# Band scores on tiles of two widths: blocks 1 and 2 as whole 128-key products

## The chip, the cores and the metric

The kernel runs on one core of a Trainium2 chip. Times are device microseconds of that core, the median of several executions; one more execution was taken with the hardware profiler, and all views of the profile come from it. PE is TensorE's matrix array (matmuls), PEld its weight loads, DVE VectorE, ACT ScalarE, POOL GpSimd, SP the engine that issues most transfers.

## The reference

The input x has the shape (2, 256, 128, 128): two items, 256 times, 128 bands, 128 channels, float32. Three residual steps follow each other, each on a layer normalization of x over the channels:

```
x = x + mha(ln(x) by time,  4 heads, causal mask over the 256 times)
x = x + mha(ln(x) by band,  4 heads, only bands at most 16 apart)
x = x + w2(gelu(w1(ln(x))))           # 128 -> 512 -> 128 channels
```

The second step is what the change touches. For each of 512 (item, time) pairs it takes 128 bands as queries and as keys. With 32 channels per head, the score of a query and a key is a dot product over 32 numbers. Scores of bands more than 16 apart are masked out before the softmax.

## The kernel before

The work is cut into groups of four blocks of 128 positions. There are three kinds: OverTime (128 groups, first), and then OverBands and FeedForward (128 groups each), which come in runs: eight OverBands groups, then their eight FeedForward groups, 16 runs in all. A group carries 512 columns of the transposed, normalized input xnT. Its stages are methods, and the loop in `run` (from line 1046) issues, for step n, the scores of group n, then the weighting (`weigh`) of group n-1, the output product of group n-2, and, for later groups, loads, statistics, normalization, and the query, key and value products. Thus a group passes through several steps, and each step of the loop mixes the stages of several groups.

The order of work on each engine is written out by hand: the class InOrder (line 860) passes each instruction to the engine and pins it to program order (line 870, which is why nearly every row of the profile names that line). So a late instruction holds up everything that stands behind it on its engine. PSUM is used as eight banks of 512 float32 columns, handed out in turn (`turn_of_bank`, line 903); a product whose bank is still being read waits for the reader.

The products run on parts of TensorE's array. A profile row such as "32*64 32x80" is a product on a tile of 32 rows and 64 columns of the array with 80 moving columns. The rows are the contraction: a head's 32 channels, so four heads sit on four row tiles. The columns are the weights' free size, here the keys. Most products of the kernel use 128*32: `product` (line 646) cuts the 128 output channels into four strips of 32. A float32 product leaves two LDWEIGHTS and two MATMUL records in the profile.

`OverBands.scores` (line 752) writes, per head, one bank with the keys on the partitions and the 512 queries of the four blocks along the columns. It works by halves of 64 keys: the first half of a block's keys reaches the block's queries 0 to 79, the second half the queries 48 to 127. The two corners that no product writes hold what stood in the bank earlier, and are masked out later. Per block there are eight products (two halves, four heads), in 32x64 tiles; per group 32.

After the scores come `first_function` (line 767): for head 3 VectorE takes the minimum with 60 and adds the band mask in place, in PSUM (`bank<-bank,band` in the profile), and ScalarE takes the exponential of each head's bank (`pf<-bank`). `first_mask` (line 777) clears, for heads 0 to 2, what lies outside the band on GpSimd. In the next step `weigh` (line 791) forms the sums of the exponentials (`bank<-pf,ones`) and the weighted values (`bank<-pf,v`); `divide` (line 615) on VectorE then inverts the sums (u) and gives oT. The next step's `output` multiplies by the output weights (`bank<-wn,oT`).

In the step after the last OverBands group of a run ("turn", line 1071) the first FeedForward group's hidden products (`bank<-xnT,w1f`) stand in front of that group's `weigh`.

The OverTime stage, which the change leaves alone, forms its scores in 32x128 tiles with 256 or 128 moving columns (`time_scores`, line 729).

Of the kernel before, what the change touches and what calls it, by code (L numbers as in the profile page):

```python
# [19 lines left out]
P = 128  # L20
H = 4
D = 32
BAND = 16
EPS = 1e-5
NEG = -1e38
NT = 4
# [6 lines left out]
HALF = P // 2  # L33
# [608 lines left out]
def rows_of(h):  # L642
    return slice(h * D, (h + 1) * D)
# [102 lines left out]
class OverBands(Attention):  # L746
# [5 lines left out]
    def scores(self, heads):  # L752
        path = self.path
        self.sp = {h: path.bank([P, NT * P], "sp") for h in heads}
        for i in range(NT):
            for e in range(2):
                keys = slice(e * HALF, (e + 1) * HALF)
                a = i * P + e * (HALF - BAND)
                q = slice(a, a + HALF + BAND)
                for h in heads:  # L760
                    r = rows_of(h)
                    path.tensor.matmul(
                        self.sp[h][keys, q], self.kT[r, i * P + e * HALF : i * P + (e + 1) * HALF], self.qT[r, q],
                        start=True, stop=True,
                    )

    def first_function(self):
# [451 lines left out]
```

## Time and profile before

| | |
|---|---|
| runs shown | median 2706.66 us of 3 (2705.89 to 2706.93) |
| the profiled execution's own time | 2703.05 us |
| its span | 2701.3 us |
| TensorE clock granted | 0.999 of full speed |
| OverTime groups, until the first band scores | 970 us |
| one run of eight OverBands and eight FeedForward groups | 107 to 108 us (the first 111) |

The span is the time between the first and the last instruction. A matmul record begins when the array starts on it; its end is modelled, and records of neighbouring products overlap. So the distance between the starts of two records tells more than their length. The idle time in brackets at the end of a timeline row is what the engine waited before it, with what released it.

### The profile page before, as it was taken

How to read it: one execution, taken by the hardware profiler on the slowest of the kernel's cores; microseconds unless marked ns; L12 is line 12 of the kernel's file. 1: busy time of each engine (PE TensorE's matmuls, PEld its weight loads, DVE VectorE, ACT ScalarE, POOL GpSimd, SP SyncE). 2: the span in 40 equal slices, each digit the busy share in tenths (PEclk: the TensorE clock that was granted, in tenths of full speed). 3: DMA queues.
4: the chain of work that ended last, by engine and by line, in shares of the span. 5: the costliest groups of instructions: out<-in, count | busy, mean ns of one | idle time of the engine just before them, and what ended most of it. 6: DMA issues, size and time to landing. Idle time of an engine off the chain costs nothing.

```text
span 2701.3 us, 148062 instructions
## 1 busy us (share of the span) xinstructions
PE 2662.7 (99%) x64566; PEld 1824.9 (68%) x64566; DVE 2280.2 (84%) x6708; ACT 1848.3 (68%) x3620; POOL 1868.7 (69%) x2169
## 2 busy tenths in 40 slices
PE   7999999999999999999999999999999999999998
PEld 5667666767676666666666666666666766666665
DVE  7999999999999997868769779688697796886874
ACT  6888888888888874655746646557456465565573
POOL 3888788878888886667657666666676666665762
PEclk9999999999999999999999999999999999999999
DMA  5555555555555535445444444454444444544433
GB/s 151 142 151 143 145 151 144 149 146 142 151 144 148 150 101 129 111 121 132 109 127 124 115 125 116 121 128 116 120 124 117 121 119 121 135 108 121 129 100 82
DMA packets 471477, 346.55 MB, mean 128 GB/s; under 512 B 43296, under 2 KB 405152, under 8 KB 470816
## 3 DMA queue, kind: packets, MB, share of 16 engines
q1 hardware_dynamic: 469568, 335.92, 47.8%
q8 instruction: 508, 8.32, 1.3%
q14 instruction: 153, 1.25, 0.2%
q10 hardware_dynamic: 1248, 1.05, 0.2%
HBM read 169.03 MB, written 167.77 MB: 125 GB/s over the span
## 4 chain that ended last, share of the span: by engine, by line
PE 83%; DVE 13%; DMA 2%; issue 1%; ACT 0%; SPq 0%; DVEq 0%; ACTq 0%
PE bank L870 83%; DVE xh L870 3%; DVE bank L870 3%; DVE stats L870 2%; DVE z L870 2%; DVE u L870 2%; DMA xnT<-turned 1%; DVE x L870 1%; DVE mv L870 1%; DMA turned<-z 0%; SPq L870 0%; DMA x<-in_x 0%; DVE oT L870 0%; DMA rows_sb<-in_rows 0%; ACT p L870 0%
## 5 line engine op out<-in xcount | busy, mean ns | idle before, releaser
L870 ACT ACTIVATE hT<-bank,b 128x512 f32<-128x512 f32 x512 | 347.1, 688 | 536.0 <-PE bank L870 517.0
L870 POOL TENSOR_SCALAR_AFFINE_SELECT pf<-pf 128x512 f32<-128x512 f32 x768 | 478.5, 638 | 246.8 <-ACT pf L870 220.5
L870 DVE TENSOR_SCALAR xh<-x,mv,rstd 128x160 f32<-128x160 f32 x1536 | 597.1, 431 | 14.2
L870 PEld LDWEIGHTS bank<-w2T_sb,hT 128*32 128x32 f32 x16384 | 459.7, 110 | 63.1 <-issue 38.8
L870 PE MATMUL bank<-xnT,wf 128*32 128x512 f32 x4096 | 488.6, 592 | 2.0 <-ACT p L870 2.0
L870 PE MATMUL bank<-w2T_sb,hT 128*32 128x128 f32 x16384 | 477.5, 273 | 0.5 <-ACT hT L870 0.2
L870 PE MATMUL bank<-xnT,w1f 128*32 128x512 f32 x4096 | 474.2, 592 | 0.0
L870 ACT ACTIVATE p<-bank 128x512 f32<-128x512 f32 (+1 forms) x1024 | 417.3, 499 | 15.1 <-PE bank L870 3.8
L870 POOL TENSOR_SCALAR_AFFINE_SELECT p<-p 128x1024 f32<-128x1024 f32 x256 | 280.9, 1097 | 188.2 <-ACT p L870 188.2
L870 DVE TENSOR_TENSOR res<-bank,res 128x512 f32<-128x512 f32 x256 | 171.1, 668 | 229.1 <-PE bank L870 227.2
L870 PE MATMUL bank<-qT,kT 32*64 32x80 f32 (+2 forms) x12288 | 346.9, 275 | 4.2 <-DVE oT L870 2.2
L870 PEld LDWEIGHTS bank<-wf,xnT 128*32 128x32 f32 x8192 | 235.5, 110 | 154.4 <-issue 135.9
L870 PEld LDWEIGHTS bank<-qT,kT 32*64 32x64 f32 (+1 forms) x12288 | 298.0, 148 | 58.7 <-ACT kT L870 48.2
L870 POOL TENSOR_TENSOR p<-p,p 128x512 f32<-128x512 f32 x256 | 329.2, 1286 | 10.7
L870 DVE BATCH_NORM_STATS2 stats<-x 128x6 f32<-128x128 f32 x1536 | 326.9, 275 | 0.9 <-DMA x<-in_x 0.9
L870 ACT ACTIVATE pf<-bank 128x512 f32<-128x512 f32 x512 | 267.1, 602 | 50.9 <-PE bank L870 48.8
L870 DVE STREAM_TRANSPOSE z<-xh 128x512 f32<-128x512 f32 x384 | 273.3, 712 | 13.4
L870 PEld LDWEIGHTS bank<-xnT,w1f 128*32 128x32 f32 x4096 | 156.4, 110 | 189.4 <-issue 159.3
L870 POOL TENSOR_SCALAR rstd<-mv 128x4 f32<-128x4 f32 x248 | 56.7, 229 | 312.8 <-DVE mv L870 311.3
L870 PE MATMUL bank<-wf,xnT 128*32 128x128 f32 x8192 | 272.6, 273 | 0.0
L870 PE MATMUL bank<-wn,oT 128*32 128x128 f32 x8192 | 271.7, 273 | 0.0
L870 POOL TENSOR_TENSOR rstd<-rstd,mhalf 128x4 f32<-128x4 f32 x248 | 257.0, 1036 | 20.7
(93 smaller groups left out, 3770.3 us busy)
## 6 DMA issues: line engine op xcount, KB each, us to landing
turned<-z SPq DMA_DIRECT2D x1536, 64.0 KB, 2.2
xnT<-turned SPq DMA_DIRECT2D x384, 256.0 KB, 3.1
x<-in_x SPq DMA_DIRECT2D x128, 256.0 KB, 4.1
x<-res SPq DMA_DIRECT2D x256, 128.0 KB, 2.4
x<-x SPq DMA_DIRECT2D x128, 256.0 KB, 4.2
out<-res SPq DMA_DIRECT2D x256, 128.0 KB, 2.5
w1T_sb<-in_w1T ACTq DMA_DIRECT2D x1, 256.0 KB, 6.5
w2T_sb<-in_w2T ACTq DMA_DIRECT2D x1, 256.0 KB, 7.9
```

The lines of the kernel that those rows point to most:

```text
L870: return self.tc.keep_in_program_order(emit(*args, **kwargs))
```

## The change

In blocks 0 and 3 of a group the scores are formed as before. In blocks 1 and 2 one product per head takes all 128 keys and all 128 queries of the block. These use tiles of 32 rows and 128 columns. A group then has 8 + 4 + 4 + 8 = 24 products, the four heads next to each other as before. No other engine's instructions, their order or their waits are edited.

```diff
     def scores(self, heads):
         path = self.path
         self.sp = {h: path.bank([P, NT * P], "sp") for h in heads}
-        for i in range(NT):
-            for e in range(2):
-                keys = slice(e * HALF, (e + 1) * HALF)
-                a = i * P + e * (HALF - BAND)
-                q = slice(a, a + HALF + BAND)
+        for i, part in ((0, HALF), (1, P), (2, P), (3, HALF)):
+            reach = 0 if part == P else BAND
+            for e in range(0, P, part):
+                a = i * P + (e - reach if e else 0)
+                q, keys = slice(a, a + part + reach), slice(i * P + e, i * P + e + part)
                 for h in heads:
                     r = rows_of(h)
                     path.tensor.matmul(
-                        self.sp[h][keys, q], self.kT[r, i * P + e * HALF : i * P + (e + 1) * HALF], self.qT[r, q],
-                        start=True, stop=True,
+                        self.sp[h][e : e + part, q], self.kT[r, keys], self.qT[r, q], start=True, stop=True
                     )
```

## The prediction

> **What bounds the kernel now.** I read the page first, then one steady step of the stage that is changed on TensorE and on VectorE, then two stages that already use what the change brings in. The page:
>
> ```profile
> span 2701.3 us, 148062 instructions
> PE 2662.7 (99%) x64566; PEld 1824.9 (68%) x64566; DVE 2280.2 (84%) x6708; ACT 1848.3 (68%) x3620; POOL 1868.7 (69%) x2169
> ...
> PE 83%; DVE 13%; DMA 2%; issue 1%; ACT 0%; SPq 0%; DVEq 0%; ACTq 0%
> ...
> L870 PE MATMUL bank<-qT,kT 32*64 32x80 f32 (+2 forms) x12288 | 346.9, 275 | 4.2 <-DVE oT L870 2.2
> ```
>
> TensorE sets the pace, VectorE takes 13% of the chain. But 99% busy does not say that PE streams all that time: a record lasts longer than the stream it stands for. The band scores are the 8,192 records of 32x80 (two for each float32 product, 64 for each of 128 groups). So I work with starts. The timeline of TensorE over one steady band step (start, length, form, count):
>
> ```profile
> 1535.81 1.09 PE L870 MATMUL bank<-qT,kT 32*64 32x80 f32 x64
> 1536.83 1.06 PE L870 MATMUL bank<-pf,ones 128*32 128x512 f32 x8
> 1537.71 1.06 PE L870 MATMUL bank<-pf,v 128*32 128x128 f32 x32
> 1538.59 1.06 PE L870 MATMUL bank<-wn,oT 128*32 128x128 f32 x32
> 1539.46 1.90 PE L870 MATMUL bank<-xnT,wf 128*32 128x512 f32 x16
> 1541.17 1.06 PE L870 MATMUL bank<-wf,xnT 128*32 128x128 f32 x32
> 1542.16 1.06 PE L870 MATMUL bank<-qT,kT 32*64 32x80 f32 x64
> ```
>
> A step is 6.35 us here; the mean of the like steps in the last 15 of the 16 runs of eight band groups is 6.324. 32 records of 128 columns take 0.88 us, four side by side in 0.109 or 0.110. Between record starts, from the last value product before the scores to the first product after them, pass 1.190 us in the mean (groups 3 to 6 of those runs; groups 0 to 2: 1.174, 1.187, 1.173).
>
> VectorE over the same step, the next one's first line included:
>
> ```profile
> 1537.32 0.69 DVE L870 SCALAR_TENSOR_TENSOR bank<-bank,band 128x512 f32<-128x512 f32 x1
> 1537.92 1.60 DVE L870 TENSOR_SCALAR xh<-x,mv,rstd 128x160 f32<-128x160 f32 x4
> ...
> 1543.24 0.69 DVE L870 TENSOR_TENSOR oT<-bank,u 128x512 f32<-128x512 f32 x1
> 1543.85 0.69 DVE L870 SCALAR_TENSOR_TENSOR bank<-bank,band 128x512 f32<-128x512 f32 x1
> ```
>
> No instruction in it has idle time before it: VectorE needs 6.53 us for a step, PE 6.32. So from the fourth group of a run VectorE falls behind. The band mask starts this long after the end of the scores, median of the 16 runs, groups 0 to 7: 0.14, 0.19, 0.21, 0.19, 0.42, 0.61, 0.83, 0.93 us. Group 7's scores then wait for banks (its stretch is 1.290 us, not 1.190), and PE waits in the turn to the feed-forward groups:
>
> ```profile
> 1562.93 0.64 PE L870 MATMUL bank<-pf,ones 128*32 128x512 f32 x4 [0.77 <-DVE u L870]
> ```
>
> Against the 430 ns of the pass before, that start is 0.95 us late; in all 16 turns 15.6 us.
>
> [...] A float32 product is two loads and two matmuls here, [...] in the group at 1510.58 us the first 32 score records run regularly and those after them come one product per about 26 ns, in steps of 17 and 42. [...]
>
> **The change, part by part.** Blocks 0 and 3 stay eight products on 32x64 tiles. Blocks 1 and 2 lose eight products of 80 columns each and get four of 128 columns on 32x128 tiles. Two changes of mode are added per group, in and out of 32x128.
>
> Price of a switch. These are its nearest rows: time stage, and the fold's end:
>
> ```profile
> 319.44 0.40 PE L870 MATMUL bank<-wf,xnT 128*32 128x128 f32 x8
> 319.77 1.62 PE L870 MATMUL bank<-qT,kT 32*128 32x128 f32 x32
> 321.32 0.42 PE L870 MATMUL bank<-p,ones 128*32 128x256 f32 x4
> ...
> 27.53 0.49 PE L870 MATMUL bank<-wf,ones 128*128 128x384 f32 x1
> 27.95 0.64 PE L870 MATMUL bank<-xnT,wf 128*32 128x512 f32 x4
> ```
>
> From the last record's start before a switch to the first after it, medians: 203 ns into 32x128 and into 32x64 after 128 columns; 200 out of 32x128 after 128 columns; 158 out of 32x64 after 80. Take off the stream (107 ns for 128 columns, 67 for 80) and 91 to 96 ns are left for each. All but one of these change the rows of the tile too. The one that changes columns only, at 27.95, takes 0.415 us after 384 columns (320 ns): 95 left. So I take 93 for each new switch. Below: nothing[...]. Above: 200, if each direction waits for the other's loads too.
>
> Exposed load. After a switch the second pass starts after stream plus first load: 120 ns in 32x64 (67 and 53), 213 in 32x128 at 128 columns (107 and 106). Once rolling, a pass of 128 columns in 32x128 takes 112, one of 80 columns in 32x64 takes 69 (eight tiles).
>
> The new stretch, from the last value product's start: into block 0, 203. Its second pass 120 later, its last tile 47 after that, out by 157: 324. Block 1, second pass, 213; block 2, two passes at 112; last tile 20; switch 200: 657. Block 3 as block 0 and out: 324. Sum 1,508 ns. Before 1,190: 318 more. [...]
>
> What this does to a run of eight groups. Groups 0 to 3 are PE's (VectorE waits 0.70 us for the scores of group 3): 334 + 321 + 335 + 318 = 1.31 us. From group 3's scores to the turn VectorE sets the time before: four steps of 6.525, 0.20 of lag, and 6.03 to the product that waits (at 1562.93 it starts 6.94 after the scores' records end at 1555.99, with a lag of 0.91): 32.33. After, a PE step is 6.324 + 0.318 = 6.642, over VectorE's 6.525: the lag stays at 0.19, the wait in group 7 goes and that in the turn falls to some 0.2. Four steps of 6.642 and 6.22 make 32.79: 0.46 more, not four times 0.318. Per run 1.77 us, 15 runs: 26.5. The first run, where refining the roots stretches VectorE's steps to 7.5 us and PE waits in five of eight groups, takes about 0.31 in each of its first two groups and hides the rest: 0.7. Sum 27.2.
>
> Covers. ACT's exponentials, POOL's masks and the band mask keep number and shape; that they read real scores where old contents of the bank stood costs no time. They start some 0.3 us later in the step, with the products that need them a step away. VectorE's step keeps 0.12 us of slack; if it had none, its 6.525 would set the step, at no more than this. Order and waits of all other engines are the same; no DMA is touched. The time stage has no edit.
>
> The sum is against the profiled execution: span 2,701.3, its own time 2,703.05, median of the runs shown 2,706.66, which lies 3.6 above. 2,706.7 + 27.2 gives 2,733.9; I say 2,733.
>
> **Rivals.**
> Forecast, chance 0.68: 2,733, its own range 2,724 to 2,742 (9 us each way are 70 ns on each of the 128 stretches).
> PE's waits stay, 0.10: they come from the order of the turn and not from the lag. 128 times 0.318 is 41: 2,747. Against it: the lag grows by 0.2 a step, as 6.53 less 6.32 says.
> Free width change, 0.10: 318 less 186 is 132; the step of 6.456 stays under VectorE's, so only groups 0 to 3 pay, 0.56 a run, about 9 in all: 2,715. Against it the 95 ns at 27.95, one instance.
> Dearer switches, 0.06: at 200 each 532 a group, four fifths of it felt: about 52, 2,759. No row speaks for it.
> Not slower, 0.06: the products are bound by their dispatch, the switches overlap it and the loads hide. Then 203, 189 for block 0, 448 for four passes, 138 and 135 out: 1,113, 77 less. Groups 4 to 7 are VectorE's, so 0.27 a run: 4 less, 2,702.5. It decides where switches and loads cost under 77 ns more than that, against 395 in my sum.
>
> **Numbers.** 2,715 to 2,748 leaves out the dear switches, the last rival and the tails. 0.2% (5.4 us) is about what a measurement of this kernel can tell from no change. Slower: the first four, 0.94, less 0.02 for a free change that ends under 5.4: 0.92. Same: 0.06, with the most of the last rival. Faster: 0.02.
>
> **What the profile after would show.** Scores of a group from 1.19 to about 1.51 us; records in 16, 16 and 16 of three stretches, 0.32 and 0.66 us apart; about 157 ns from the last 80-column start to the first 128. The band mask's lag about 0.2 us in group 7, the wait for u at the turn about 0.2 us; the step 6.64. Wrong, if the new switches show under 50 or over 150 ns, if the lag still grows, or if a new wait stands in the feed-forward steps.

## The result and the profile after

The changed kernel takes 2732.35 us (median of 6), against 2705.89 us (6 runs beside it): 1.0096 times as long, 95% interval 1.0083 to 1.0109, 26.5 us slower. 2,733 was forecast, by 27.2 us of addition to 2,706.7 (2,733.9, given as 2,733). The page of the changed kernel:

```profile
span 2731.0 us, 143966 instructions
PE 2704.0 (99%) x62518; PEld 1826.6 (67%) x62518; DVE 2284.8 (84%) x6708; ACT 1845.0 (68%) x3620; POOL 1864.1 (68%) x2169
...
PE 88%; DVE 10%; DMA 1%; ACT 0%; issue 0%; POOL 0%; SPq 0%; DVEq 0%; ACTq 0%
...
L869 PE MATMUL bank<-qT,kT 32*64 32x80 f32 (+2 forms) x10240 | 386.6, 295 | 3.6 <-DVE oT L869 2.2
```

The matmul records fall by 2,048, two for each of 8 products less in 128 groups. Yet the score records (the line also holds those of the time stage, which are unchanged) cover 386.6 us, and not 346.9, and VectorE's share of the chain falls from 13 to 10%: more of the chain runs over PE. One steady step on TensorE, timeline:

```profile
1547.71 1.38 PE L869 MATMUL bank<-qT,kT 32*64 32x80 f32 x48
1549.02 1.06 PE L869 MATMUL bank<-pf,ones 128*32 128x512 f32 x8
...
1553.36 1.06 PE L869 MATMUL bank<-wf,xnT 128*32 128x128 f32 x32
1554.35 1.38 PE L869 MATMUL bank<-qT,kT 32*64 32x80 f32 x48
```

(The view joins the 32 records of 32x80 and the 16 of 32x128 in one line under the first one's form.) From the first score to the first product after the scores, 1.31 us pass; in the kernel before it was 1.02 (1535.81 to 1536.83). The rest of the step is as it was. The step is 6.64 us. What is called the stretch below goes from the start of the last value product before the scores to the start of the first product after them. In this group its parts are 203 ns into block 0, then 324 to block 1, 656 to block 3 and 325 out: 1,508 ns in all. Over the last 15 runs of eight groups the mean stretch is 1,507 or 1,508 ns in seven of the eight places. From the last 80-column record to the first of 128 it is 157 or 158 ns in all 128 groups, and 200 ns on the way back.

VectorE in that step, timeline:

```profile
1549.34 0.70 DVE L869 SCALAR_TENSOR_TENSOR bank<-bank,band 128x512 f32<-128x512 f32 x1
...
1555.27 0.69 DVE L869 TENSOR_TENSOR oT<-bank,u 128x512 f32<-128x512 f32 x1
1556.01 0.70 DVE L869 SCALAR_TENSOR_TENSOR bank<-bank,band 128x512 f32<-128x512 f32 x1
```

Its step is now 6.67 us in this place (6.64 in the mean from group 4 on), 6.53 before: the band mask starts 0.74 us after oT, and no longer 0.61, because it has to wait for the scores. The band mask's lag, from the end of the score records to its start, is 0.28 us in groups 1 to 7 alike (median), where it grew to 0.93. And the wait in the turn is mostly gone. The timeline line that answers to the one at 1562.93 has no idle time in brackets, and starts 0.33 us late against the pass before it, where that one was 0.95 late:

```profile
1575.32 0.64 PE L869 MATMUL bank<-pf,ones 128*32 128x512 f32 x4
```

The lists of PE's waits over the whole span (total us, times, longest) say the same in one number, first before, then after:

```profile
PE bank L870 <- DVE u L870: 13.2, 17, 0.8
```

```profile
PE bank L869 <- DVE u L869: 1.4, 5, 0.7
```

**Where the time went.** The profiled executions are 29.7 us apart (2731.0 and 2701.3). Of this 3.0 lie ahead of the first band scores, where nothing was changed; they are not the change's (last section). The first run of eight and eight groups takes 0.6 us more, the next 14 runs 1.74 each in the mean (107.38 to 109.12), the last, with the end, 1.73: 26.7 in all, close to the 26.5 of the timed runs.

### The profile page after: what moved, and what is told of

It is laid out like the page before. It is cut to its first block, busy times and chain, and to the rows that moved or that the text cites. A ratio compares the mean times of both kernels' runs of the same rounds, so it can differ in the third digit from the quotient of the medians.

```text
span 2731.0 us, 143966 instructions
## 1 busy us (share of the span) xinstructions
PE 2704.0 (99%) x62518; PEld 1826.6 (67%) x62518; DVE 2284.8 (84%) x6708; ACT 1845.0 (68%) x3620; POOL 1864.1 (68%) x2169
## 4 chain that ended last, share of the span: by engine, by line
PE 88%; DVE 10%; DMA 1%; ACT 0%; issue 0%; POOL 0%; SPq 0%; DVEq 0%; ACTq 0%
PE bank L869 87%; DVE xh L869 2%; DVE bank L869 2%; DVE stats L869 1%; DVE u L869 1%; DVE z L869 1%; DVE x L869 1%; DVE oT L869 1%; DMA xnT<-turned 1%; DVE mv L869 0%; ACT p L869 0%; POOL pf L869 0%; DMA f_wiT_sb<-in_f_wiT 0%; ACT pf L869 0%; DVE vy L869 0%
## 5 line engine op out<-in xcount | busy, mean ns | idle before, releaser
L869 PE MATMUL bank<-qT,kT 32*64 32x80 f32 (+2 forms) x10240 | 386.6, 295 | 3.6 <-DVE oT L869 2.2
L869 PEld LDWEIGHTS bank<-qT,kT 32*128 32x128 f32 (+1 forms) x10240 | 311.2, 163 | 85.3 <-ACT kT L869 49.0
L869 PEld LDWEIGHTS bank<-xnT,w1f 128*32 128x32 f32 x4096 | 150.5, 110 | 193.9 <-issue 168.7
L869 ACT ACTIVATE qT<-bank,bq 128x512 f32<-128x512 f32 x256 | 176.1, 688 | 132.1 <-PE bank L869 131.8
```

The costliest lines, as they stand in the source:

```text
L869: return self.tc.keep_in_program_order(emit(*args, **kwargs))
```

## The experiments

They ask three things: is it the changes of mode that cost, or the wide products; what are eight products fewer worth; and did VectorE's lag hide a part of the price? Each stretch below is the mean or median over the last 15 runs, from the starts of the records.

**All blocks whole.** No change of mode inside a group.

```diff
-        for i, part in ((0, HALF), (1, P), (2, P), (3, HALF)):
+        for i, part in ((0, P), (1, P), (2, P), (3, P)):
```

> All four blocks as whole products on 32x128 tiles: 16 products, no change of mode inside the group. If each change of mode costs about 93 ns over the stream and one exposed load (my theory), the stretch from the last value product to the first product after the scores is 203 + 213 + 6 x 112 + 20 + 200 = 1,308 ns, 200 less than in the changed kernel though two more blocks are whole; the step is 6.44 us, below VectorE's 6.525, so only groups 0 to 3 of a run pay: 0.51 us a run, about 8 us over before (2,714). If the whole products are dear in themselves, as 328 ns for each of blocks 1 and 2 in the changed kernel reads, the stretch stays about 1,515 ns and the time at that of the changed kernel, 2,732.

Measured: 1,306 ns, step 6.44 us, 2710.33 us against 2705.32 (1.0018, interval 1.0012 to 1.0025): 5.0 over before. Four wide blocks take 200 ns less than two. So the wide products are not what is dear. The addition is 3 us smaller than expected: a run takes 0.37 us more than before, not 0.51, and the missing part is in group 0, as in the changed kernel ("Groups 0 to 3" below).

**Wide blocks first.** The same 24 products, one change of mode fewer.

```diff
-        for i, part in ((0, HALF), (1, P), (2, P), (3, HALF)):
+        for i, part in ((1, P), (2, P), (0, HALF), (3, HALF)):
```

> The same 24 products, blocks 1 and 2 first and then 0 and 3: one change of mode fewer inside the group. Theory of the switches: 203 + 457 + 200 + 305 + 157 = 1,322 ns, step 6.46 us, 0.56 us a run for groups 0 to 3 alone, about 9 us over before (2,715). If the products themselves cost it, the order does not matter: 1,508 ns and 2,732.

Measured: 1,322 ns (1,443 in group 2, with a wait), step 6.45, 2715.18 us (1.0038, 1.0024 to 1.0052): 9.9 over before. The order alone takes 186 ns off a group and 17 us off the kernel. 186 is more than one switch: next to each other, blocks 0 and 3 save, beside its 90 ns, one exposed load (53 ns, an estimate: 120 to the second pass less 67) and one offset of the eight tiles' starts (47 ns).

**Wide and narrow by turns.** The same products, one change of mode more than in the changed kernel (five in place of four, those into and out of the scores included).

```diff
-        for i, part in ((0, HALF), (1, P), (2, P), (3, HALF)):
+        for i, part in ((1, P), (0, HALF), (2, P), (3, HALF)):
```

> The same 24 products in the order 1, 0, 2, 3: two more changes of mode than in the changed kernel. Theory of the switches: 203 + 433 + 324 + 433 + 324 = 1,717 ns, 209 more than the changed kernel; PE's step is 6.85 us, over VectorE's, so nearly all of it is felt: some 26 us over the changed kernel, 52 over before (2,758). If the products themselves cost it: 1,508 ns and 2,732.

The sum is right, but against the changed kernel the order has one change more, not two; two more is its distance from the order with the wide blocks first. Measured: 1,717 ns, step 6.85, 2758.54 us (1.0198, 1.0181 to 1.0215): 53 over before, 26 over the changed kernel. One change is worth 209 ns here. TensorE's timeline of one such group:

```profile
1559.38 1.06 PE L869 MATMUL bank<-wf,xnT 128*32 128x128 f32 x32
1560.37 1.58 PE L869 MATMUL bank<-qT,kT 32*128 32x128 f32 x48
1561.88 1.07 PE L869 MATMUL bank<-pf,ones 128*32 128x512 f32 x8
```

The same 48 score records now take 1.51 us from the first start to the next product, 1.31 in the changed kernel. The three experiments together leave no room for the theory that the products cost it.

**24 products without a change of mode.** The kernel before, without the second key half of blocks 1 and 2.

```diff
-            for e in range(2):
+            for e in range(2 if i in (0, 3) else 1):
```

> The kernel before with the second key half of blocks 1 and 2 left out (those scores are not computed): 24 products in one mode, which asks what eight products fewer are worth alone. [...] the stretch falls from 1,190 to about 1,000 ns, though the array still streams eight passes of 69 ns; groups 0 to 3 gain 0.7 us a run, groups 4 to 7 nothing, because VectorE sets their time: about 11 us under before (2,695). If the number of products means nothing: 1,190 ns, 2,706.

Measured: 993 to 1,013 ns in groups 0, 1 and 3 to 5 (1,042 in group 2), 1,325 and 1,387 in groups 6 and 7; 2693.87 us (0.9958, 0.9941 to 0.9974): 11.5 under before. The array streams as many passes here as before: the four remaining products of blocks 1 and 2 stand on the same tile columns, and their passes start 69 ns apart, four records at a time. So what the missing products save, about 190 ns, is not the time of passes. It fits the irregular records: outside groups 6 and 7 the first 32 of the 48 records run regularly (over 417 ns in the median), and the intervals of 16 and 17 ns begin only after them, as after the first 32 of 64 in the group at 1510.58 us of the kernel before. Eight passes without a stop would sum to 941 ns (203 + 120 + 6 x 69 + 47 + 157), so some 50 to 70 ns of it are left. In the changed kernel all 48 records run regularly (outside group 2, 4,469 of 4,480 intervals within a pass are 6 or 7 ns). What makes the later records irregular was not shown. And the lag of VectorE now bounds the second half of a run sooner: its median is 0.62 us in group 4 and 1.04 in group 5. PE's waits for u grow:

```profile
PE bank L870 <- DVE u L870: 16.1, 17, 1.0
```

**VectorE out of the way.** In both kernels the cap and mask of head 3 are left out.

```diff
-        for h in range(H - self.by_vector, H):
+        for h in ():
```

> The kernel before without the band mask of head 3 on VectorE (that head's scores are neither capped nor masked): VectorE's step falls by 0.6 us to about 5.9, below PE's 6.32. If VectorE's lag is what makes PE wait in group 7, in the turn and in the first run, these waits go: (0.10 + 0.97) x 15 and some 4 us in the first run, about 20 us under before (2,686). If the waits come from the order of the turn, little changes: 2,700 to 2,706.

> The changed kernel without the band mask of head 3 on VectorE, to be compared with the kernel before without it. With VectorE out of the way the whole price of the scores should be felt: 128 x 0.318 = 41 us between the two (about 2,727 against 2,686), in place of 27. If VectorE had hidden nothing, the difference stays 27.

Measured: without the mask the kernel before takes 2688.48 us (0.9940 of the kernel before, 0.9925 to 0.9955), 16.7 under it where some 20 were expected; the changed one takes 2726.35 (1.0076, 1.0060 to 1.0091). Between the two lie 37.9 us, not 26.5. In the traces a run of groups takes 106.47 and 108.80 us: 2.33 us apart, where it is 1.74 with the mask. The start after the turn is no longer late in either. The head of the list of PE's waits in the first of them:

```profile
PE bp L870 <- DMA cols_sb<-in_cols: 3.6, 1, 3.6
PE bank L870 <- ACT orow L870: 2.8, 2, 1.9
PE bank L870 <- ACT p L870: 2.0, 2, 1.2
PE bank L870 <- DVE oT L870: 1.9, 1, 1.9
...
PE bank L870 <- DVE u L870: 0.7, 1, 0.7
```

One wait for u is left, of 0.7 us; in the kernel before they head the list, with 13.2 us. So about 11 us of the scores' price are hidden by VectorE's lag. That it is not the full 41 lies mostly in group 0, whose step grows by 0.14 us in this pair and not by 0.33 (7.39 to 7.53), much as with the mask. Groups 4 and 5 of the kernel before have longer steps without the mask (6.39 and 6.36 us in the mean, 6.33 with it; one group 4 has a stretch of 1,872 ns), which takes another 0.1 us; the late entry to group 2's scores gives most of that back. Over groups 0 to 6 the steps of the kernel before are 0.14 us a run longer without the mask, so its own gain falls short of the 20 us too. The cause of that is open.

**The lag relieved in the kernel before.** Here all is computed; GpSimd masks head 3 in two of eight groups.

```diff
-                for g, part, load, _ in run:
-                    yield OverBands(self, partial(part, "x", g), partial(part, "x2", g), partial(load, g))
+                for n, (g, part, load, _) in enumerate(run):
+                    group = OverBands(self, partial(part, "x", g), partial(part, "x2", g), partial(load, g))
+                    group.by_vector = 0 if n in (4, 6) else 1
+                    yield group
```

> The kernel before with head 3's band mask on GpSimd, as for the other heads, in groups 4 and 6 of each run. VectorE's lag loses 1.2 us by group 7, so it stays near 0.2, and PE's waits in group 7 and in the turn (1.07 us a run together) fall to some 0.2: about 13 us under before (2,693). GpSimd takes 1.28 us more in these two steps, 6.3 of 6.33: if it comes late, PE waits for the masked exponentials and the gain is lost, 2,706 or more.

Measured: 2692.76 us (0.9954, 0.9940 to 0.9968), 12.5 under before and 40 under the changed kernel: faster than both. The start after the turn is 0.24 to 0.35 us late in the last 15 runs, in place of about 0.95. Group 7 takes 1,172 ns, in place of 1,290. GpSimd's timeline in groups 6 and 7 of a run:

```profile
1549.78 5.24 POOL L870 TENSOR_SCALAR_AFFINE_SELECT pf<-pf 128x512 f32<-128x512 f32 x8 [0.82 <-ACT pf L870]
1555.00 0.23 POOL L870 TENSOR_SCALAR rstd<-mv 128x4 f32<-128x4 f32 x1
1555.32 1.04 POOL L870 TENSOR_TENSOR rstd<-rstd,mhalf 128x4 f32<-128x4 f32 x1
1556.56 3.94 POOL L870 TENSOR_SCALAR_AFFINE_SELECT pf<-pf 128x512 f32<-128x512 f32 x6 [0.20 <-ACT pf L870]
```

The eight masks (six in the next group) are done before the next group's exponentials are: GpSimd has idle time before them both times (0.82 and 0.20 us), so the room was there.

## Why the prediction was right, step by step

**The stretch of the scores.** Forecast 1,508 ns, measured 1,508. The switch was put at 93 ns over the stream. It is 90 or 91 into the wide tiles (157 or 158 less 67 for 80 columns) and 93 out of them (200 less 107 for 128 columns); 67 and 107 are estimates from the 430 ns that a pass of 512 columns takes. The row that carried it, the one change of width at 27.95 us, had shown 95. The exposed loads, 53 ns and 106 or 107, are estimates too, from the starts of the second passes (120 less 67, and 213 or 214 less 107); in the group at 1547.71 us the second set of weight loads starts 55 ns after the first in the narrow tiles and 108 in the wide ones. Four arrangements of the same pieces came out at 1,306, 1,322, 1,508 and 1,717 ns, where the sums gave 1,308, 1,322, 1,508 and 1,717. So pass, exposed load, tile offset and switch add up.

**The irregular records.** The sum of 1,508 ns counts nothing for eight products fewer, and that was right: the new stretch repeats to the nanosecond (1,507 or 1,508 outside group 2), without the spread of the old one (1,098 to 1,250 ns in groups 0 to 6 of the last 15 runs). 24 products in one mode show what the irregular records had been worth, up to the 50 to 70 ns that they keep of it.

**Groups 0 to 3.** Forecast 1.31 us a run, measured 1.21. The step of group 0 takes 0.17 more, not 0.33: in the kernel before this step varied from 7.16 to 7.75 us, in the changed one it is 7.525 or 7.526 every time. In one of the long ones (at 2158 us) the weight loads stand 0.37 us with nothing that the profile names; stops of this length are not in this step after. Not every long step has one, so why group 0 pays only half stays open. The stretch of group 2 takes 0.42 more, not 0.34, by a wait that the prediction did not have: the exponentials start later, the copy of the next keys stands behind them on ScalarE, and the weight loads wait for it.

```profile
1533.81 0.57 ACT L869 COPY kT<-bank 128x512 f32<-128x512 f32 x1
1534.43 0.75 PEld L869 LDWEIGHTS bank<-qT,kT 32*64 32x64 f32 x28 [0.25 <-ACT kT L869]
```

These are ScalarE and the weight loads in one such group of the changed kernel; the entry to the scores takes 0.25 us there and 0.29 in the mean of 15 runs, not 0.20. My covers put the later start of the exponentials, some 0.3 us, at nothing. Here it costs 0.08 to 0.09 us in each of 15 runs. Reading real scores in place of old contents left the lengths about as they were: the exponentials take 602 ns before and 603 after in the mean, GpSimd's masks 638 and 635, the band masks 690 and 700 in the median.

**Groups 4 to 7 and the turn.** Forecast 0.46 us, measured 0.52: the step is 6.637 (6.642), the lag stops at 0.28 and not at 0.19 (the cause is open), and the start in the turn is 0.33 late and not 0.2. The sum of a run is 1.73 to 1.74 against 1.77. The first run takes 0.6 (0.7). That the total fits within 1 us is in part luck: 0.16 us too much for group 0 stands against 0.15 too little for group 2 and for groups 4 to 7 with the turn.

**The rivals.** That the waits stay fell with the list of waits and with the pair without the mask. The free change of width fell with the 90 and 93 ns. The dearer switch fell with them too. The one that ends without a loss needed switches and loads at under 77 ns together; they cost 395, as summed.

## What to carry to other kernels

Count changes of mode (from one form of tile to another) before products: in this kernel each cost some 146 ns into the narrow tiles and 197 into the wide ones, about as much as two passes of the scores (69 and 112 ns each). By estimate from the starts of the records, 93 and 90 of it are the switch and 53 and 107 the first load that nothing covers. So order products by mode, and give up a smaller shape where it needs a switch of its own. And before a cost is multiplied by its number of places, look which engine sets the time at each: here VectorE's step of 6.53 us and PE's of 6.32 took turns within a run of eight, and of what was added to the faster one 26.5 us were felt, against 37.9 without the band mask.

## What the runs showed of the hardware

The 3.0 us ahead of the band scores go with a stretch at half clock. At the seam between the two stages PE waits 1.9 us in both kernels (first before, then after):

```profile
963.91 0.71 PE L870 MATMUL bank<-qT,kT 32*128 32x128 f32 x8 [1.87 <-DVE oT L870]
```

```profile
963.72 1.23 PE L869 MATMUL bank<-qT,kT 32*128 32x128 f32 x8 [1.86 <-DVE oT L869]
```

In the profile of the changed kernel it is granted half its clock from then on (windows: length, busy times, granted clock, transfer share and GB/s):

```profile
963.70:965.00 1.30, 1.28 (x12) 1.06 (x16) 1.30 (x10) 0.02 (x1) 1.30 (x2) 0.50 0.01 4
965.00:970.40 5.40, 5.40 (x72) 3.42 (x76) 1.89 (x5) 1.86 (x4) 4.61 (x4) 0.50 0.37 97
970.40:975.00 4.60, 4.60 (x120) 2.76 (x114) 3.24 (x8) 2.38 (x6) 0.22 (x1) 1.00 0.41 99
```

The clock's record gives it 6.83 us. In five of the seven experiments there is such a stretch of 3.41 us at the same seam, and in the profile of the kernel before and two experiments none, with the same code there. The first band scores start at 970.1 to 970.7 us in the three profiles without it, at 972.1 to 973.0 in the five, and at 973.3 here. Half clock follows PE's wait in six of nine profiles, and the kernel before waits as long (1.87 us) without it. So the wait alone does not decide it; what does was not shown.

The timed runs of one kernel spread over 2 to 6 us. With all blocks whole, 13 of them with a mean granted clock of 0.999 took 2707.9 to 2710.6 us, and 7 with 0.998 took 2711.6 to 2712.7; the five runs of the last experiment are not sorted so. Where in a timed run the clock was lower is not on record. That filling the seam would end it was not tried.
